# Decoder layer on one core: the opening's diagonal operands made early, its second rounds dense, its stores and loads in another order

## The chip, the core and the metric

One core of one Trainium2 chip runs the whole kernel. TensorE (PE) multiplies matrices into PSUM, VectorE (DVE), ScalarE (ACT) and GpSimd (POOL) work elementwise, and SyncE (SP) issues the DMA transfers. Each engine runs its own instructions in order and waits on semaphores for the others. The metric is the device time of one execution in microseconds (us), lower is better.

## The reference

The input `x` is (4, 2048, 512) in float32, with a context of 77 tokens for each of 4 batches. Three sublayers add to `x` in turn, each on its layer norm:

```python
x = x + recurrence(layernorm(x))            # diagonal state space along the FIRST axis, 4 steps, blocks of 64 features
x = x + cross_attention(layernorm(x), ctx)  # 16 heads of 32, 77 keys, softmax, output projection
x = x + ffn(layernorm(x))                   # 512 -> 2048, butterfly, gelu, butterfly, 2048 -> 512
```

A butterfly is a product of 11 sparse stages (2048 = 2^11), each mixing pairs of features at distance 1, 2, 4, ... 1024. It is linear, so the kernel multiplies `W_exp` with the up butterfly, and the down butterfly with `W_con`, once at the start, and has two dense matrices after that.

## The kernel before, in words

The second axis of `x` is cut into 16 tiles of 128 positions, each with all 4 steps of the first axis. A loop runs over the tiles: `feed_forward` of one tile is interleaved on TensorE with `front` of the next (recurrence, attention and three norms). Dense products use a scheme of seven products for a 2 x 2 block product; so each weight is stored as seven quarter-sized operands: three plain quarters and four sums, in DRAM tensors `up7` (8 blocks of hidden features), `dn7` (7 operands) and `wq7`.

Ahead of the loop stands the opening, which is where the change lies. It holds three generators, each of which emits some instructions up to its next `yield`; calls of `run(...)` (L783) and the loop at L802 decide which comes next. TensorE and SyncE run strictly in that written order (`manual_schedule`, L765). The order on VectorE, ScalarE and GpSimd is made by a planner that works with estimated times; only instructions under `keep` stay in order there.

- `taps` (L68) makes the recurrence matrices `gt`: four rounds, where each L111/L112 product waits for VectorE's L128 to L131.
- `keys` (L135) makes the keys (L146, evicted at L150) and values (L156).
- `prep` is `_prepare` (L220). It makes the two dense matrices. The up matrix: products of the low 7 stages (`_low_products`, L181) and of the high 4 stages (`_high_products`, L206), then a first round of products with the low stages (L282) into `wup`, transposes (L291) into `wdn`, and a second round with the high stages (L304), whose right operands are 16 "diagonals": 128 x 128 blocks that spread the high products over a mask (L244). The results go to `up7`: three plain quarters for each of 8 blocks are stored from `wup` (L326, 24 stores of 128 KB), and four sums made by GpSimd (L321, L323) and VectorE (L322, L324) in the buffer of `wo`, three slots in turn, are stored with one transfer each (L327, 8 stores of 512 KB). `W_con` is loaded (L310) into `wdn` as each group of the second round is done with it. The down matrix: a second round first (L340, with its own 16 diagonals), transposes (L350), low stages (L359), then sums (L370 to L373) and stores (L375) into `dn7`.
- `first` is `front(0)` (L495): the first tile's norm, recurrence, norm, seven query products `q` (L490), scores (L548), softmax (L552 to L558), transposes of the probabilities (L570), outputs (L580), seven output products `w` (L490), and the norm before the feed-forward (L446).

Buffers are shared by tags. `pt`, the transposed probabilities (L566), has the tag of the query weights `wq` (L777), so that the first copy into it (L575) has to wait until the store of `wq` (L801) has been read out. `wup` is overwritten by the second round of the down matrix, so an eviction there waits for the stores and sums that still read the up matrix. The feed-forward's buffers (`xlast`, `wts`, `ffn`, L820 to L822) lie where the opening's pool `prep` was, and the first of their users wait for all of that pool's last readers.

The pieces that the change touches and what calls them:

## Time and profile before

| | us |
|---|---|
| median of 3 runs (lowest, highest) | 2680.2 (2679.2, 2681.05) |
| the profiled execution's own time | 2681.39 |
| its span, first to last instruction | 2679.6 |
| first product of the feed-forward (L649) starts at | 265.69 |
| mean granted TensorE clock | 0.985 |

Busy times of the span: TensorE 2586.2 (97%), VectorE 1454.6 (54%), ScalarE 810.2 (30%), GpSimd 947.8 (35%). A line of a timeline reads: start, duration, engine, line of the kernel, operation, output<-inputs, shape, count, and in brackets the idle time of the engine just before and what ended it. A group's line gives busy time and the mean of one in ns. A chain's line gives start, duration and what it was. L12 is line 12 of the kernel before.

### The profile page before, as it was taken

How to read it: one execution, taken by the hardware profiler on the slowest of the kernel's cores; microseconds unless marked ns; L12 is line 12 of the kernel's file. 1: busy time of each engine (PE TensorE's matmuls, PEld its weight loads, DVE VectorE, ACT ScalarE, POOL GpSimd, SP SyncE). 2: the span in 40 equal slices, each digit the busy share in tenths (PEclk: the TensorE clock that was granted, in tenths of full speed). 3: DMA queues.
4: the chain of work that ended last, by engine and by line, in shares of the span. 5: the costliest groups of instructions: out<-in, count | busy, mean ns of one | idle time of the engine just before them, and what ended most of it. 6: DMA issues, size and time to landing. Idle time of an engine off the chain costs nothing.

```text
span 2679.6 us, 37402 instructions
## 1 busy us (share of the span) xinstructions
PE 2586.2 (97%) x14536; PEld 2197.8 (82%) x14536; DVE 1454.6 (54%) x3349; ACT 810.2 (30%) x1470; POOL 947.8 (35%) x1023
## 2 busy tenths in 40 slices
PE   7876999999999999999999999999999999999999
PEld 4755888888888888888888888888888888888888
DVE  5466555556455455645545654655555564554541
ACT  1322332414132332414133241413324141323321
POOL 4043252433425242342515234341524334252423
PEclk9978999999999999999999999999999999999999
DMA  5255324243332424233242423334242433324234
GB/s 176 81 169 175 128 92 159 93 156 108 105 139 91 162 95 158 91 134 130 85 148 94 171 93 118 130 103 146 93 158 93 156 108 105 140 91 146 95 128 139
DMA packets 92595, 333.60 MB, mean 124 GB/s; under 512 B 15362, under 2 KB 44162, under 8 KB 75266
## 3 DMA queue, kind: packets, MB, share of 16 engines
q1 hardware_dynamic: 92418, 331.21, 35.8%
q8 instruction: 116, 1.90, 0.3%
q14 instruction: 61, 0.49, 0.1%
HBM read 297.61 MB, written 33.57 MB: 124 GB/s over the span
## 4 chain that ended last, share of the span: by engine, by line
PE 82%; DVE 6%; ACT 4%; issue 1%; DMA 1%; SPq 0%; ACTq 0%; DVEq 0%
PE ps_a L716 12%; PE ps_b L649 10%; PE ps_b L716 8%; PE ps_w L490 7%; PE ps_a L649 7%; PE ps_c L649 7%; PE ps_q L490 7%; PE ps_c L716 6%; PE ps_sc L548 4%; PE ps_pt L570 4%; PE ps_s L505 3%; PE ps_o L580 2%; PE ps_t L446 2%; ACT L554 1%; ACT L654 1%; DVE st L411 1%
## 5 line engine op out<-in xcount | busy, mean ns | idle before, releaser
L649 PE MATMUL ps_b<-tb,w_up 128*128 128x256 f32 x1536 | 397.8, 380 | 0.0
L716 PE MATMUL ps_a<-w_dn,a 128*128 128x256 f32 x1536 | 373.0, 380 | 0.0
L692 POOL TENSOR_TENSOR s<-a,a 128x256 f32<-128x256 f32 x128 | 92.8, 725 | 676.7 <-ACT a L654 454.2
L649 PEld LDWEIGHTS ps_b<-tb,w_up 128*128 128x128 f32 x1536 | 288.0, 191 | 39.3 <-issue 0.2
L654 ACT ACTIVATE a<-a,hbias 128x256 f32<-128x256 f32 x384 | 193.6, 508 | 407.4 <-DVE a L687 277.6
L716 PEld LDWEIGHTS ps_a<-w_dn,a 128*128 128x128 f32 x1536 | 282.7, 190 | 41.3 <-issue 3.0
L649 PE MATMUL ps_a<-xnt,w_up 128*128 128x256 f32 x1024 | 263.9, 380 | 8.7 <-DMA w_up<-up 8.7
L716 PE MATMUL ps_c<-w_dn,s 128*128 128x256 f32 x1024 | 248.7, 379 | 0.0
L558 POOL TENSOR_TENSOR pr<-pr,sm 128x1232 f32<-128x1232 f32 x64 | 143.9, 2249 | 272.3 <-DVE sm L557 234.1
L447 ACT COPY xnt<-ps_t 128x512 f32<-128x512 f32 x128 | 73.5, 587 | 525.6 <-PE ps_t L446 525.6
L649 PEld LDWEIGHTS ps_a<-xnt,w_up 128*128 128x128 f32 x1024 | 191.9, 191 | 34.5 <-POOL ybias L819 9.1
L716 PEld LDWEIGHTS ps_c<-w_dn,s 128*128 128x128 f32 x1024 | 189.0, 190 | 27.5
L548 PE MATMUL ps_sc<-kbd,qt 128*128 128x308 f32 x512 | 176.3, 442 | 7.9 <-DVE pr L553 7.6
L598 DVE TENSOR_TENSOR xt<-ps_w,xt 128x512 f32<-128x512 f32 x96 | 66.1, 689 | 213.8 <-PE ps_w L490 144.9
L704 POOL TENSOR_TENSOR xt<-xt,ybias 128x256 f32<-128x256 f32 x128 | 99.2, 807 | 223.3 <-DVE xn L437 223.2
L570 PE MATMUL ps_pt<-ident,pr 128*77 128x128 f32 x1024 | 146.1, 279 | 9.5 <-ACT a L654 3.6
L570 PEld LDWEIGHTS ps_pt<-ident,pr 128*77 128x77 f32 x1024 | 118.8, 149 | 43.8 <-ACT a L654 11.0
L554 ACT ACTIVATE pr<-pr 128x308 f32<-128x308 f32 x256 | 111.6, 457 | 132.9 <-DVE pr L553 132.4
L490 PE MATMUL ps_q<-xnt,wq 128*128 128x256 f32 x640 | 151.3, 380 | 0.0
L490 PEld LDWEIGHTS ps_q<-xnt,wq 128*128 128x128 f32 x640 | 121.4, 190 | 16.2
L649 PE MATMUL ps_c<-tb,w_up 128*128 128x256 f32 x512 | 132.3, 381 | 0.0
L649 PE MATMUL ps_c<-xnt,w_up 128*128 128x256 f32 x512 | 131.5, 379 | 0.0
(202 smaller groups left out, 4531.2 us busy)
## 6 DMA issues: line engine op xcount, KB each, us to landing
w_up<-up SPq DMA_DIRECT2D x128, 896.0 KB, 4.6
w_dn<-dn SPq DMA_DIRECT2D x112, 1024.0 KB, 4.8
wq<-wq SPq DMA_DIRECT2D x16, 1792.0 KB, 8.4
xt<-in_x SPq DMA_DIRECT2D x16, 1024.0 KB, 5.4
out<-xt SPq DMA_DIRECT2D x64, 256.0 KB, 4.8
wdn<-in_wexp_t SPq DMA_DIRECT2D x4, 1024.0 KB, 10.3
wdn<-in_wcon SPq DMA_DIRECT2D x4, 1024.0 KB, 5.0
up<-wo SPq DMA_DIRECT2D x8, 512.0 KB, 3.9
```

The source lines that it names most:

```text
L447: nc.scalar.copy(xnt[:, :, t, :], ps)
L490: nc.tensor.matmul(tiles[key][:, r, :], lhsT=lhs(i, r, k), rhs=rhs(i, r, k), start=key == i and r == 0 and k == 0, stop=k == 1, skip_group ...
L505: nc.tensor.matmul(ps[:, 2 * i : T, f * NS : (f + 1) * NS], lhsT=xpt[:, i, c * (P // NS) + f, :], rhs=gt[:, 0 : T - 2 * i, :], start=i == ...
L548: nc.tensor.matmul(ps[:, 0 : 4 * NK], lhsT=qt[:, g, t, :], rhs=kbd[:, t, g, :], start=True, stop=True)
L554: nc.scalar.activation(pg, pg, AF.Exp, scale=1.0 / math.sqrt(DH))
L558: nc.gpsimd.tensor_tensor(pr, pr, sm.unsqueeze(2).to_broadcast([P, NH, NK]), ALU.mult)
L570: nc.tensor.transpose(pt_ps[0:NK, j, :], pr[:, 4 * g + j, :], ident)
L649: nc.tensor.matmul(ps, lhsT=w[:, c, :], rhs=rhs[i - 1][:, c], start=first and c == 0, stop=c == 1, skip_group_check=True)
L654: nc.scalar.activation(out, x, AF.Gelu, bias=hbias[:, b : b + 1])
L692: nc.gpsimd.tensor_tensor(s1, a21, a22, ALU.add)
L704: nc.gpsimd.tensor_tensor(r, r, ybias[:, d], ALU.add)
L716: nc.tensor.matmul(ps[:, t, :], lhsT=act[p][lhs[i]][:, t, :], rhs=w[:, p, :], start=first and p == 0 and t == 0, stop=p == h - 1, skip_gro ...
```

## The change

- The 16 diagonals of each matrix are made by one call, all at once: those of the up matrix ahead of the transposes L291, into the buffer of `wo`; those of the down matrix after the second round of the up matrix, into the buffer that held the keys' weights (tag `xt1`). The buffer `more` and the use of `ybias` for them go.
- The four groups of the second round L304 follow each other with nothing of `first` between. The second round L340 runs with its loops exchanged (`c` outside, `g` inside) and gives way to `first` after every group.
- The high products of both matrices and the low products of the down matrix move to earlier places; `low_dn` is loaded earlier.
- The 24 stores of plain quarters are all issued ahead of the sums and their 8 stores. The store of `wq` comes after those.
- The sums and stores of `dn7` are made in four parts of 2 blocks instead of two parts of 4 (stores of 256 KB).
- The loads at the start are reordered (`x` after the keys' operands and the low coefficients), the tile `x` of the second position is loaded earlier, and the steps of the three generators are interleaved in another order; one step of `prep` is now one group instead of four.
- The pools `ffn` and `wts` change places.

```diff
+    yield
...
-        yield
...
         pz = nxt
+        yield
...
     nc.sync.dma_start(out=wk, in_=wk_t.rearrange("(c p) e -> p c e", p=P))
+    yield
     nc.sync.dma_start(out=wv, in_=wv_t.rearrange("(c p) e -> p c e", p=P))
...
-    def diagonal(hp, m, place):
-        bd = place.rearrange("p (b i) -> p b i", b=NB)
-        keep(nc.vector.tensor_tensor(bd, hp[:, m, :].unsqueeze(2).to_broadcast([P, NB, sub]),
-                                     mask.unsqueeze(1).to_broadcast([P, NB, sub]), ALU.mult))
-        return bd.rearrange("p b i -> p (b i)")
+    def diagonals(hp, place):
+        for m in range(NB):
+            keep(nc.vector.tensor_tensor(place[:, m, :].rearrange("p (b i) -> p b i", b=NB),
+                                         hp[:, m, :].unsqueeze(2).to_broadcast([P, NB, sub]),
+                                         mask.unsqueeze(1).to_broadcast([P, NB, sub]), ALU.mult))
+        return [place[:, m, :] for m in range(NB)]
...
-        nc.sync.dma_start(out=high, in_=coefs)
+    for i, coefs in enumerate((up_high, dn_high)):
+        nc.sync.dma_start(out=highs[:, i], in_=coefs)
     half = NB * 2 * (P // 2 - 1)
     nc.sync.dma_start(out=low[:, 0:half], in_=up_low[:, 0:half])
     nc.sync.dma_start(out=low[:, half:nlow], in_=up_low[:, half:nlow])
+    yield
...
+    hp = _regrouped(nc, keep, pool, hscr[0], _high_products(nc, pool, highs[:, 0], False), "hp_up")
     e = _low_products(nc, keep, low, False, True)
-    hp = _regrouped(nc, keep, pool, hscr[0], _high_products(nc, pool, highs[0], False), "hp_up")
+    hp_dn = _high_products(nc, pool, highs[:, 1], True)
     yield
...
     nc.sync.dma_start(out=bias, in_=up_bias)
+    nc.sync.dma_start(out=brow[0:1, :], in_=brw.rearrange("o g x -> o (g x)"))
...
         yield
-    nc.sync.dma_start(out=brow[0:1, :], in_=brw.rearrange("o g x -> o (g x)"))
-    hp_dn = _regrouped(nc, keep, pool, hscr[1], _high_products(nc, pool, highs[1], True), "hp_dn")
+    nc.sync.dma_start(out=b2, in_=brow[0, :].rearrange("(p m) -> p m", m=NB))
+    low = pool.tile([P, nlow], F32, tag="lowc", name="low_dn")
+    keep(nc.sync.dma_start(out=low, in_=dn_low))
+    hp_dn = _regrouped(nc, keep, pool, hscr[1], hp_dn, "hp_dn")
+    bd = diagonals(hp, spare[:, 0 : NB * P].rearrange("p (m q) -> p m q", q=P))
...
-    low = pool.tile([P, nlow], F32, tag="lowc", name="low_dn")
-    keep(nc.sync.dma_start(out=low, in_=dn_low))
-    nc.sync.dma_start(out=b2, in_=brow[0, :].rearrange("(p m) -> p m", m=NB))
+    el = _low_products(nc, keep, low, True, False)
     pb = banks()
     for g in range(4):
-        bd = [diagonal(hp, 4 * g + j, room3[:, (4 * g + j) * P : (4 * g + j + 1) * P]) for j in range(4)]
         for c in range(NC):
...
                 nc.tensor.matmul(ps.rearrange("p (k m) -> p m k", m=4)[:, j], lhsT=t[:, 4 * g + j, c * P : (c + 1) * P],
-                                 rhs=bd[j], start=j == 0, stop=True, skip_group_check=True)
+                                 rhs=bd[4 * g + j], start=j == 0, stop=True, skip_group_check=True)
...
     nc.vector.tensor_copy(b2, pb[:, 0:NB])
-    nc.sync.dma_start(out=brow[1, :].rearrange("(p m) -> p m", m=NB), in_=b2)
+    bdd = diagonals(hp_dn, late())
     h, k = HID // 2, NC // 2
-    for p in range(NB // 2):
+
+    def quarters(p):
         q = slice(p * P, (p + 1) * P)
         a11, a12 = wup[:, 0:k, q], wup[:, k:NC, q]
         q = slice(h + p * P, h + (p + 1) * P)
-        a21, a22 = wup[:, 0:k, q], wup[:, k:NC, q]
-        s = room3[:, p % 3 * 1024 : p % 3 * 1024 + 1024].rearrange("p (i k q) -> p i k q", i=4, k=k)
-        nc.gpsimd.tensor_tensor(s[:, 0], a21, a22, ALU.add)
-        nc.vector.tensor_tensor(s[:, 1], s[:, 0], a11, ALU.subtract)
-        nc.gpsimd.tensor_tensor(s[:, 2], a11, a21, ALU.subtract)
-        nc.vector.tensor_tensor(s[:, 3], a12, s[:, 1], ALU.subtract)
+        return a11, a12, wup[:, 0:k, q], wup[:, k:NC, q]
+
+    for p in range(NB // 2):
+        a11, a12, a21, a22 = quarters(p)
         for i, a in enumerate((a11, a12, a22)):
             nc.sync.dma_start(out=up7[p][:, i], in_=a)
+    for p in range(NB // 2):
+        a11, a12, a21, a22 = quarters(p)
+        s = spare[:, p % 3 * 1024 : p % 3 * 1024 + 1024].rearrange("p (i k q) -> p i k q", i=4, k=k)
+        nc.gpsimd.tensor_tensor(s[:, 0], a21, a22, ALU.add)
+        nc.gpsimd.tensor_tensor(s[:, 2], a11, a21, ALU.subtract)
+        nc.vector.tensor_tensor(s[:, 1], s[:, 0], a11, ALU.subtract)
+        nc.vector.tensor_tensor(s[:, 3], a12, s[:, 1], ALU.subtract)
         nc.sync.dma_start(out=up7[p][:, 3:7], in_=s)
-        if p % 2:
-            yield
-    e = _low_products(nc, keep, low, True, False)
-    more = sums[0].tile([P, 8, P], F32, name="more")
-    places = [more[:, i] for i in range(8)] + [room4[:, i * P : (i + 1) * P] for i in range(4)]
-    places += places[0:4]
-    yield
-    for g in range(4):
-        bd = [diagonal(hp_dn, 4 * g + j, places[4 * g + j]) for j in range(4)]
-        for c in range(NC):
+        yield
+    nc.sync.dma_start(out=brow[1, :].rearrange("(p m) -> p m", m=NB), in_=b2)
+    for c in range(NC):
+        for g in range(4):
             ps = banks()
             for j in range(4):
                 nc.tensor.matmul(ps.rearrange("p (k m) -> p m k", m=4)[:, j], lhsT=t[:, 4 * g + j, c * P : (c + 1) * P],
-                                 rhs=bd[j], start=j == 0, stop=True, skip_group_check=True)
+                                 rhs=bdd[4 * g + j], start=j == 0, stop=True, skip_group_check=True)
             evict(wup[:, c, :].rearrange("p (k m) -> p k m", m=NB)[:, :, 4 * g : 4 * g + 4], ps.rearrange("p (k m) -> p k m", m=4))
-        yield
+            yield
...
-        nc.tensor.matmul(ps, lhsT=e[:, b, :], rhs=t[:, b, :], start=True, stop=True)
+        nc.tensor.matmul(ps, lhsT=el[:, b, :], rhs=t[:, b, :], start=True, stop=True)
         evict(wdn[:, b, :], ps)
-        if n % 2:
-            yield
         if n == h:
             nc.sync.dma_start(out=b1, in_=brow[1, :].rearrange("(b p) -> p b", p=P))
-        if n % h == h - 1:
-            f = slice(n // h * (h // 2), (n // h + 1) * (h // 2))
-            b11, b12, b21, b22 = (wdn[:, r * h + f.start : r * h + f.stop, c * (D // 2) : (c + 1) * (D // 2)].rearrange("p (x b) d -> p x b d", x=2)
+        if n % 4 == 3:
+            f = slice(n // 4 * 2, n // 4 * 2 + 2)
+            b11, b12, b21, b22 = (wdn[:, r * h + f.start : r * h + f.stop, c * (D // 2) : (c + 1) * (D // 2)]
                                   for r in range(2) for c in range(2))
-            t1, t2, t3, n4 = (wup[:, i, :].rearrange("p (x y) -> p x y", x=2)[:, :, n // h * D : (n // h + 1) * D] .rearrange("p x (b d) -> p x b d", b=2) for i in range(4))
+            t1, t2, t3, n4 = (wup[:, i, :].rearrange("p (x y) -> p x y", x=2)[:, :, f.start * P : f.stop * P] for i in range(4))
             nc.vector.tensor_tensor(t1, b12, b11, ALU.subtract)
             nc.gpsimd.tensor_tensor(t3, b22, b12, ALU.subtract)
             nc.vector.tensor_tensor(t2, b22, t1, ALU.subtract)
             nc.vector.tensor_tensor(n4, b21, t2, ALU.subtract)
             for i, w in ((0, b11), (1, b21), (2, b22), (4, t1), (6, t3), (5, t2), (3, n4)):
-                nc.sync.dma_start(out=dn7[i][:, f, :].rearrange("p (x b) d -> p x b d", x=2), in_=w)
+                nc.sync.dma_start(out=dn7[i][:, f, :], in_=w)
+        yield
     keep(nc.vector.tensor_tensor(bias, b1, bias, ALU.add))
     yield
...
-                        up_bias, dn_low, dn_high, wcon, wup, wdn, hbias, up7, dn7)
+        rooms = high, row, wo.rearrange("p i k d -> p (i k d)")
+        prep = _prepare(nc, tc.keep_in_program_order, pool, rooms, lambda: xpool.tile([P, NB, P], F32, tag="xt1", name="bd"),
+                        banks, dram, ident, wexp_t, up_low, up_high, up_bias, dn_low, dn_high, wcon, wup, wdn, hbias, up7, dn7)
         room = (work.tile([P, NC, T * NK], F32, tag="pr", name="ct"), xpool.tile([P, NC, D], F32, tag="xt1", name="wk"),
...
+            for g in gens:
+                next(g, None)
+
+        def quarter_loads(w, w_t, places):
+            src = w_t.rearrange("(c p) e -> p c e", p=P)
+            for i, (c, e) in zip(places, ((0, 0), (1, 0), (1, 1), (0, 1))):
+                nc.sync.dma_start(out=w[:, i], in_=src[:, 2 * c : 2 * c + 2, e * (D // 2) : (e + 1) * (D // 2)])
+
         with tc.tile_pool(name="taps", bufs=1) as tp:
             taps = _recurrence_taps(nc, tp, psum, ssm_vec, ssm_vt, ssm_vinv, gt)
+            run(taps, keys, prep, keys)
             xts[0] = load_x(0)
+            next(prep)
+            quarter_loads(wq, wq_t, (0, 1, 3, 6))
             first = front(0, xts.pop(0), ready, wq)
-
-            def run(*gens):
-                for g in gens:
-                    next(g, None)
-
-            run(taps, keys, prep)
-            src = wq_t.rearrange("(c p) e -> p c e", p=P)
-            for i, (c, e) in ((0, (0, 0)), (1, (1, 0)), (3, (1, 1)), (6, (0, 1))):
-                nc.sync.dma_start(out=wq[:, i], in_=src[:, 2 * c : 2 * c + 2, e * (D // 2) : (e + 1) * (D // 2)])
-            run(first, keys, keys, taps, keys, keys, taps, keys, keys, taps, taps)
-        sums.append(stack.enter_context(tc.tile_pool(name="sums", bufs=1)))
-        run(first, keys, first, keys, first, first, prep, first, first, first, first)
+            run(keys, keys, taps, keys, taps, first, keys, taps, keys, taps, keys, first, keys, first)
+            run(prep, first, keys, first, first)
+        run(first, first, first, first)
         nc.gpsimd.tensor_tensor(wq[:, 4], wq[:, 6], wq[:, 3], ALU.add)
         nc.gpsimd.tensor_tensor(wq[:, 6], wq[:, 0], wq[:, 6], ALU.subtract)
         nc.gpsimd.tensor_tensor(wq[:, 5], wq[:, 4], wq[:, 0], ALU.subtract)
         nc.gpsimd.tensor_tensor(wq[:, 2], wq[:, 1], wq[:, 5], ALU.subtract)
-        run(prep, prep, first, prep, first, first, prep, first, first)
+        run(prep, prep, first, prep, first, prep, first)
+        run(prep, first, prep, first, prep, first, prep)
         run(prep, prep, prep, prep)
-        run(first, first, first, prep, first, first, prep, first, first, prep, first, first, prep)
+        for _ in range(8):
+            run(first, prep)
         nc.sync.dma_start(out=wq7, in_=wq)
+        run(first, first, first)
         for n, _ in enumerate(prep):
-            for _ in range(1 + (n < 4)):
+            if n % 3 != 2 or n > 14:
                 next(first, None)
-            if n == 4:
-                src = wo_t.rearrange("(c p) e -> p c e", p=P)
-                for i, (c, e) in ((0, (0, 0)), (1, (1, 0)), (2, (1, 1)), (6, (0, 1))):
-                    nc.sync.dma_start(out=wo[:, i], in_=src[:, 2 * c : 2 * c + 2, e * (D // 2) : (e + 1) * (D // 2)])
+            if n == 3:
+                quarter_loads(wo, wo_t, (0, 1, 2, 6))
                 nc.gpsimd.tensor_tensor(wo[:, 4], wo[:, 6], wo[:, 0], ALU.subtract)
                 nc.gpsimd.tensor_tensor(wo[:, 6], wo[:, 2], wo[:, 6], ALU.subtract)
                 nc.gpsimd.tensor_tensor(wo[:, 5], wo[:, 2], wo[:, 4], ALU.subtract)
                 nc.gpsimd.tensor_tensor(wo[:, 3], wo[:, 1], wo[:, 5], ALU.subtract)
-        xts[1] = load_x(1)
+            if n == 18:
+                xts[1] = load_x(1)
         for _ in first:
             pass
         db = work.tile([P, D], F32, tag="xn", name="db")
@@ -818,8 +829,8 @@
         nc.sync.dma_start(out=db, in_=down_bias.partition_broadcast(P))
         nc.gpsimd.tensor_tensor(ybias, ybias, db, ALU.add)
     xlast = ctx.enter_context(tc.tile_pool(name="xlast", bufs=1))
+    ffn = ctx.enter_context(tc.tile_pool(name="ffn", bufs=2))
     wts = ctx.enter_context(tc.tile_pool(name="wts", bufs=3))
-    ffn = ctx.enter_context(tc.tile_pool(name="ffn", bufs=2))
```

## The prediction

> **What bounds the kernel now.** I read the page's slices first: TensorE stands at 9 tenths everywhere but in the first three or four of the 40 slices (67 us each), so the loop over the 16 tiles is TensorE's, and only the opening, up to the first product of the feed-forward at 265.69 us, has room. From that product on both programs run the same instructions in the same order, except that the second tile's first transposes move. So I cut the opening into six stages by TensorE's order and asked for busy time by stage (columns: stretch, length, then PE, PEld, DVE, ACT, POOL busy, granted clock, DMA share, GB/s):
>
> ```profile
> 0.00:58.20 58.20, 40.74 (x153) 24.92 (x154) 27.49 (x119) 5.85 (x10) 29.23 (x82) 0.97 0.60 200
> 58.20:86.98 28.78, 28.78 (x249) 27.04 (x248) 18.34 (x39) 19.36 (x27) 1.03 (x1) 1.00 0.27 83
> 86.98:135.50 48.52, 37.62 (x217) 32.86 (x217) 19.55 (x39) 10.14 (x17) 5.45 (x6) 0.86 0.19 66
> 135.50:209.86 74.36, 52.35 (x346) 40.02 (x346) 46.56 (x82) 15.44 (x29) 34.77 (x30) 0.72 0.45 152
> 209.86:243.67 33.81, 33.42 (x154) 22.95 (x152) 19.48 (x27) 11.42 (x21) 7.12 (x4) 1.00 0.35 110
> 243.67:265.69 22.02, 3.77 (x17) 3.04 (x17) 18.28 (x44) 2.92 (x5) 7.44 (x6) 0.65 0.96 320
> ```
>
> Call them A (taps, keys, recurrence), B (first round, transposes), C (second round of the up matrix, L304), D (attention with the down matrix's second round, L340), E (its transposes and last products) and F (last stores, first weights). B and E are full; A, C, D and F have holes. In C the timeline shows whose:
>
> ```profile
> 103.77 3.84 PE L304 MATMUL ps_p<-wo,wdn 128*128 128x128 f32 x32 [0.98 <-DVE wo L244]
> 107.45 0.95 PE L309 MATMUL ps_p<-b,wo 128*128 128x1 f32 x8
> ...
> 113.03 3.81 PE L304 MATMUL ps_p<-wo,wdn 128*128 128x128 f32 x32 [1.07 <-DVE wo L244]
> ...
> 126.44 0.71 PE L304 MATMUL ps_p<-wo,wdn 128*128 128x128 f32 x4 [3.48 <-DVE wo L244]
> ```
>
> Each group of four blocks waits for its diagonals (L244), then takes 4.46 us (113.03 to 117.49, L309 included). The costs of a diagonal, by group on VectorE in 120 to 210 us:
>
> ```profile
> L244 DVE TENSOR_TENSOR more<-hp_dn,mask 128x128 f32<-128x128 f32 x12 | 9.9, 883 | 0.0
> ...
> L244 DVE TENSOR_TENSOR ybias<-hp_dn,mask 128x128 f32<-128x128 f32 x4 | 0.9, 284 | 0.0
> ```
>
> Alone four take 0.9 us; beside a GpSimd operation one takes 0.9. In D the attention starts late for another reason, which the timelines of the DMA queue and VectorE and the table of transfers show (start, us, instruction):
>
> ```profile
> 135.28 0.42 SPq L801 DMA_DIRECT2D wq<-wq  x1
> 146.33 2.05 SPq L326 DMA_DIRECT2D up<-wup  x3
> 145.45 0.69 DVE L575 COPY pt<-ps_pt 77x512 f32<-77x512 f32 x1 [0.25 <-DMA up<-wup]
> wq<-wq SPq DMA_DIRECT2D x1, 1792.0 KB, 10.1
> ```
>
> `pt` lies in `wq`'s buffer, so the first copy of transposed probabilities (L575) can't run before the store of `wq` (L801) has landed: 135.28 + 10.1 = 145.4. In F the chain is one of stores and loads:
>
> ```profile
> 244.62 3.12 DVE wup L370
> ...
> 250.37 6.52 DMA dn<-wup
> ...
> 257.35 8.34 DMA w_up<-up
> ```
>
> **The change part by part.** Times from the start of a stage.
>
> **A, 58.2 to 51.5.** `x` (1 MB) leaves the head of the queue: the keys' operands come about 3 us sooner, and their products run first, at 8.3 instead of 12.9 us. One key product (3 us) now stands between each recurrence step and the next tap, hiding the three waits of 2.03, 2.03 and 1.07 us for L130. Against it: the second row of `xp` takes `high`'s buffer, free only after GpSimd's last L206, which waits behind the `wq` loads (36.5 us, same bytes as before): about 41 us, a hole of 2. Sum -6.7.
>
> **B, 28.8 to 30.3.** All 16 diagonals of the up matrix go to VectorE just before the evictions of L291: 16 x 0.22 = 3.6 us, of which the free PSUM banks cover some two: +1.5. Loading `low_dn` and its products (9.2 us of GpSimd) come here and into C; GpSimd was idle there, and evictions from PSUM took 0.69 us beside these products in D (176.24), so they cost nothing.
>
> **C, 48.5 to 17.8.** Four groups of 4.46 us, no diagonals, no attention between: -30.7. Six of the seven `q` products and the first scores, which lay in C, are only moved on into D.
>
> **D, 74.4 to 91.** The long one; offsets from its start.
> - VectorE makes the 16 down diagonals while GpSimd does six L321/L323 (0.73) and L534 (1.26), 5.7 us. The Trainium skill ("SBUF — State Buffer", SBUF: two separate sides) says that the pair of ports is locked for a whole instruction and a VectorE operation with two SBUF inputs blocks. Row: 0.93 us a diagonal beside GpSimd (3.86 for four at 183.75), not 0.22. By the row nine diagonals and the first `q` sum end at 7.6, where by uncontended rows it would be 3; by the rule, full blocking, 9. I take the row. The later products wait for these sums in one PSUM tile: scores start at 16, two rows of four at 0.97 each end at 25 with the row sum (1.44).
> - Queue: 24 stores of plain quarters now stand ahead of the eight stores of sums. Three took 2.05, so 24 x 0.70 = 16.8, plus 2 behind the last `wcon` load: the first sums' store goes at 19 and lands 3.9 later. GpSimd: L558 of row 0 from 23.2 to 25.5, three pairs of sums to 30, L558 of row 1 to 35.5, two last pairs to 38.3; last L324 at 39.0, its store at 39.2, and only then L801 at 39.8. It needs 8 us (10.1 in the crowded queue, 8.4 for the load of that size; 5 at the peak of 437 GB/s; I take the nearest): 48.
> - Behind that wait: VectorE's and ScalarE's first `pt` copies, hence everything in their queues. From the same copy to the last row sum took 145.45 to 170.31 = 24.9 us; less ten L322/L324 (5.5), plus three evictions (2.1): 21.5, so 69.5.
> - Left for TensorE: two rows of transposes and outputs (6.0), eight groups of L340 (7.5), two `w` products (3.5), copies waited for (1.5): 88.
> - The clock: the skill ("TensorE: Matmul & The Clock Gate", Part 1) says that after an idle window of about 3.4 us the array runs at half speed until busy as long. D is emptier than before. Row: 0.72 granted in D. By the rule alone the last 18 us would double at worst (+18), by the row +7; a burst of L340 (3.83 us for 32, as warm) shows that it recovers, so I take +3: 91.
> - Loads of `wo` queue behind L801 and land at about 51; their four sums (1.26 each) end at 56, before L558 of row 2 (59): hidden by 3 us.
>
> **E, 33.8 to 39.5.** TensorE has 31 us left, two `w` products being done, and the four transposes of `xn` come in. But the last L598 ends at 17, and between it and the first `xn` row VectorE's queue now holds 12 us: six L411 at 0.65 (the second tile's among them), four evictions at 0.69, one and a half quarters' sums and the Newton steps. `xn` comes at 29.5, then 10 us of products: 39.5. Before, this norm lay in F under the stores.
>
> **F, 22.0 to 15.5.** Half-size sums: last eviction 0.6, three of 0.69 beside one GpSimd 1.26: 3.3 (before 5.6). The last store has 256 KB: 3.5, as the 128 KB ones took, instead of 6.52. `x` no longer precedes `w_up`: 4.6 is the median of its loads, but the second tile's four transposes, which wait for GpSimd's L819, now stand first: 8.1. These (2.4 us) leave the loop.
>
> **Other places for weights**: nothing; the first `w_up` still waits for every last `dn7` store, in either layout.
>
> New opening 51.5 + 30.3 + 17.8 + 91 + 39.5 + 15.5 = 245.6, against 265.7: -20.1, with the moved transposes -22.5. From the span 2679.6 that gives 2657.1. The profiled run took 2681.4, the median is 2680.2, so I add 0.6 to a span: **2658**.
>
> **The rivals.**
> - *The store queue becomes the bound (slower).* At 139.48 three such stores took 6.27 us behind L801. For: eight outstanding transfers are all the queue has. Against: L801 no longer lies among them. At 2.1 us each, 24 take 50: D grows by 33 and the kernel ends at 2691. It decides from 1.6 us a store (24 x 0.9 = 22). Chance 0.12.
> - *D and E are nearer to their parts.* If the sums run ahead, L801 goes at 33, and if the norm's instructions fit between evictions (E 34): 16 less, from 2628 to 2645, centre 2640. For: VectorE was busy only 63% of D. Chance 0.22.
> - *The gain comes back in D.* Clock by its row, `wo` sums late before L558, D at 103 to 108: 2672 to 2680. For: clock 0.72. Chance 0.16.
> - *It doesn't do what it says*: if the diagonals were not the reason for C's holes, C stays at 26 or so: inside the first range.
>
> **How the numbers follow.** 0.2% (5.4 us, about what a measurement tells from no change) puts "same" at 2675 to 2686. My case, 2645 to 2672, has 0.50: faster. The second is faster. Of the third half is faster, half same. The first is slower, the same slowness also coming from smaller mishaps of its kind. Faster 0.80, same 0.08, slower 0.12. Range 2632 to 2682: below it about 0.07, above 0.12.
>
> **What would show it.** Right: L304 in one run of about 18 us without waits for L244; L272 near 51; L801 issued some 40 us after the last L309, with the first L575 waiting for it; the first `w_up` product near 246. Wrong: L801 landing before 42 or after 55; a clock under 0.6 in D; no stall on `xn` in E; C over 22.

## The result, and the profile after

The changed kernel takes 2663.98 us (median of 4 runs, 2662.71 to 2665.23) against 2680.2 us: a ratio of 0.994, with a 95% interval of 0.9922 to 0.9957. That is 16 us faster; 2658 (2632 to 2682) was forecast. Its profiled span is 2662.7 us (before 2679.6), at a granted TensorE clock of 0.987 (before 0.985).

The code of the changed kernel stands up to twelve lines lower. The lines that matter below, before > after: taps L116 > L117 and L124 the same (VectorE's read of `ps_g`, TensorE's product `ps_ri`), keys L146 > L148, start of the first round L272 > L277, the diagonals L244 > L248 (L244 is now ScalarE's eviction), second rounds L304 > L310 and L340 > L346, the bias products L309 > L315, plain quarters' stores L326 > L331, sums' stores L327 > L339, transposes and low stages of the down matrix L350 and L359 > L356 and L365, its sums L370 to L373 > L374 to L377 and stores L375 > L379, scores L548 > L553, GpSimd's softmax product L558 > L563, first copy of `pt` L575 > L580, store of `wq` L801 > L812, addition of the biases L819 > L830, first feed-forward product L649 > L654.

The same cut of the opening into stages A to F by TensorE's order, busy time by stage of the changed kernel (columns as before: stretch, length, PE, PEld, DVE, ACT, POOL busy, granted clock, DMA share, GB/s):

```profile
0.00:59.15 59.15, 43.62 (x153) 25.23 (x153) 33.80 (x119) 5.75 (x10) 28.94 (x82) 0.91 0.59 197
59.15:89.23 30.08, 28.88 (x250) 27.17 (x250) 21.80 (x56) 19.55 (x28) 3.78 (x5) 1.00 0.26 79
89.23:107.01 17.78, 17.78 (x162) 17.78 (x161) 4.86 (x8) 6.21 (x11) 8.58 (x6) 1.00 0.53 179
107.01:192.99 85.98, 55.06 (x418) 43.84 (x418) 51.84 (x97) 19.86 (x37) 32.16 (x29) 0.84 0.40 133
192.99:234.47 41.48, 34.64 (x153) 23.62 (x151) 30.89 (x75) 12.51 (x22) 5.84 (x4) 0.88 0.46 145
234.47:253.14 18.67, 5.03 (x19) 3.74 (x20) 10.85 (x14) 2.93 (x5) 10.67 (x11) 0.58 1.01 327
```

| stage | before | predicted | after | after minus predicted |
|---|---|---|---|---|
| A | 58.2 | 51.5 | 59.2 | +7.7 |
| B | 28.8 | 30.3 | 30.1 | -0.2 |
| C | 48.5 | 17.8 | 17.8 | 0 |
| D | 74.4 | 91 | 86.0 | -5.0 |
| E | 33.8 | 39.5 | 41.5 | +2.0 |
| F | 22.0 | 15.5 | 18.7 | +3.2 |
| from the first L654 to the end | 2413.9 | 2411.5 | 2409.6 | -1.9 |

So C became dense and D longer, as forecast, and the total is near; but A gained nothing. Before, TensorE had three waits for L130 in A, of 2.03, 2.03 and 1.07 us; here the first of them and what follows it:

```profile
22.96 0.43 PE L111 MATMUL ps_g<-vt,pz_next 64*128 64x64 f32 x2 [2.03 <-DVE ti L130]
...
23.70 6.10 PE L146 MATMUL ps_k<-ct,wk 128*128 128x308 f32 x16
29.74 0.43 PE L122 MATMUL ps_rr<-pz_next,vt 64*64 64x128 f32 x2
```

In the changed kernel TensorE's timeline shows new waits, and VectorE's timeline what it did in the meantime:

```profile
19.77 0.40 PE L124 MATMUL ps_ri<-pz,vt 64*64 64x128 f32 x2 [1.43 <-DVE gt L117]
25.25 0.40 PE L124 MATMUL ps_ri<-pz_next,vt 64*64 64x128 f32 x2 [1.43 <-DVE gt L117]
25.80 4.03 PE L148 MATMUL ps_k<-ct,wk 128*128 128x308 f32 x8
33.33 0.66 PE L124 MATMUL ps_ri<-pz_next,vt 64*64 64x128 f32 x2 [2.33 <-DVE gt L117]
34.34 6.24 PE L158 MATMUL ps_v<-wv,ct 128*77 128x512 f32 x8
```

```profile
17.21 1.94 DVE L152 COPY kbd<-ps_k 32x308 f32<-32x308 f32 x4 [0.83 <-PE ps_k L148]
19.16 0.46 DVE L117 TENSOR_SCALAR gt<-ps_g 64x64 f32<-64x64 f32 x2
```

The three waits for L130 are gone, and three for L117 (5.19 us together, against 5.13) stand in their place. `ps_g`, `ps_rr` and `ps_ri` share one PSUM tag with two buffers. So `ps_ri` needs the one that VectorE still has to read for `ps_g`, and that read stands behind the key product's four copies (the third time with the norm's small steps between them). Before, a key product (23.70 above) lay between `ps_g` and `ps_rr` and hid the read; the moved `yield` puts it behind `ps_ri`. The products after the second and third wait ran at half clock (4.03 against 2.34 us for the same eight, 6.24 against 3.60).

In D, the timelines of the DMA queue and of VectorE show the order that was forecast, somewhat earlier:

```profile
106.88 15.15 SPq L331 DMA_DIRECT2D up<-wup  x24
122.17 21.45 SPq L339 DMA_DIRECT2D up<-wo  x8
143.66 0.44 SPq L812 DMA_DIRECT2D wq<-wq  x1
```

```profile
151.44 0.69 DVE L580 COPY pt<-ps_pt 77x512 f32<-77x512 f32 x1 [8.21 <-DMA wq<-wq]
```

The store of `wq` goes 36.7 us after D's start and lands at 151.4, which is what the first copy of `pt` waits for, and TensorE waits for the copies:

```profile
152.12 1.99 PE L575 MATMUL ps_pt<-ident,pr 128*77 128x128 f32 x8 [16.30 <-ACT pt L578]
```

In E the transposes of `xn` wait 6.69 us for VectorE (221.44). In F VectorE's timeline has two waits on the way to the first product:

```profile
242.86 1.80 DVE L624 TENSOR_TENSOR tb<-xnt 128x512 f32<-128x512 f32 x1 [4.60 <-DMA ybias<-in_b_con]
...
248.15 3.11 DVE L469 TENSOR_SCALAR xp<-xt,mv,y 128x256 f32<-128x256 f32 x4 [1.16 <-POOL ybias L830]
```

The first is the opening's pool coming free with the last stores (the first `w_up` is issued at 242.56). The bracket names the load of `ybias`, but that lands only 4.8 us after its issue at 239.35; what had just landed is the last store (242.3). The second is the second tile's rows `xp`: the bias `db` lies in one of the two buffers that they use, until L830 has read it. The last transpose is at 251.40, the first L654 at 253.14.

### The profile page after: what moved, and what is told of

The parts are those of the page before. It is cut to its first block, busy times and chain, and to the rows that moved or that the text cites. A ratio compares the mean times of both kernels' runs of the same rounds, so it can differ in the third digit from the quotient of the medians.

```text
span 2662.7 us, 37427 instructions
## 1 busy us (share of the span) xinstructions
PE 2570.4 (97%) x14536; PEld 2183.1 (82%) x14536; DVE 1453.5 (55%) x3355; ACT 810.1 (30%) x1470; POOL 949.7 (36%) x1025
## 4 chain that ended last, share of the span: by engine, by line
PE 83%; DVE 6%; ACT 4%; issue 1%; DMA 0%; POOL 0%; SPq 0%; ACTq 0%; DVEq 0%; POOLq 0%
PE ps_a L721 13%; PE ps_b L654 10%; PE ps_b L721 8%; PE ps_w L495 7%; PE ps_a L654 7%; PE ps_c L654 7%; PE ps_q L495 7%; PE ps_c L721 6%; PE ps_sc L553 5%; PE ps_pt L575 4%; PE ps_s L510 3%; PE ps_o L585 2%; PE ps_t L451 2%; ACT L559 1%; DVE st L416 1%
## 5 line engine op out<-in xcount | busy, mean ns | idle before, releaser
L654 PE MATMUL ps_b<-tb,w_up 128*128 128x256 f32 x1536 | 396.8, 379 | 0.0
L654 PEld LDWEIGHTS ps_b<-tb,w_up 128*128 128x128 f32 x1536 | 287.4, 190 | 39.3
L654 PE MATMUL ps_a<-xnt,w_up 128*128 128x256 f32 x1024 | 263.6, 380 | 0.0
L563 POOL TENSOR_TENSOR pr<-pr,sm 128x1232 f32<-128x1232 f32 x64 | 144.0, 2250 | 263.0 <-DVE sm L562 259.0
L654 PEld LDWEIGHTS ps_a<-xnt,w_up 128*128 128x128 f32 x1024 | 191.7, 191 | 25.7
L709 POOL TENSOR_TENSOR xt<-xt,ybias 128x256 f32<-128x256 f32 x128 | 99.3, 810 | 223.0 <-DVE xn L442 222.9
L553 PE MATMUL ps_sc<-kbd,qt 128*128 128x308 f32 x512 | 172.6, 434 | 5.1 <-DVE pr L558 4.8
L575 PE MATMUL ps_pt<-ident,pr 128*77 128x128 f32 x1024 | 145.7, 278 | 29.0 <-ACT pt L578 17.8
L575 PEld LDWEIGHTS ps_pt<-ident,pr 128*77 128x77 f32 x1024 | 118.9, 149 | 61.7 <-ACT pt L578 26.4
L654 PE MATMUL ps_c<-xnt,w_up 128*128 128x256 f32 x512 | 131.5, 379 | 0.0
L654 PE MATMUL ps_c<-tb,w_up 128*128 128x256 f32 x512 | 131.5, 379 | 0.0
```

Of the source, the lines that this page charges most:

```text
L553: nc.tensor.matmul(ps[:, 0 : 4 * NK], lhsT=qt[:, g, t, :], rhs=kbd[:, t, g, :], start=True, stop=True)
L563: nc.gpsimd.tensor_tensor(pr, pr, sm.unsqueeze(2).to_broadcast([P, NH, NK]), ALU.mult)
L575: nc.tensor.transpose(pt_ps[0:NK, j, :], pr[:, 4 * g + j, :], ident)
L654: nc.tensor.matmul(ps, lhsT=w[:, c, :], rhs=rhs[i - 1][:, c], start=first and c == 0, stop=c == 1, skip_group_check=True)
L709: nc.gpsimd.tensor_tensor(r, r, ybias[:, d], ALU.add)
```

## The experiments

Each kernel is the changed one with one edit (g_bank_hp has two, the combos three or four), timed against the kernel before. Ratios have an interval of about 0.0013 to either side (0.0007 for dn_diag_group, 0.0018 for the changed kernel). Stages come from TensorE's timeline of each profile, cut at the same instructions as above, but with C up to the end of the last L315, which lies 0.14 us later. Kernels with moved lines have their own numbers in their rows.

| kernel | median us | ratio to before | A | C | D | E | F | rest |
|---|---|---|---|---|---|---|---|---|
| changed | 2663.98 | 0.9940 | 59.1 | 17.9 | 85.8 | 41.5 | 18.7 | 2409.6 |
| g_bank | 2658.25 | 0.9915 | 52.3 | 17.9 | 89.5 | 40.7 | 18.7 | 2409.1 |
| g_bank_hp | 2657.10 | 0.9912 | 50.2 | 17.9 | 87.2 | 40.6 | 18.6 | 2409.5 |
| diag_group | 2667.79 | 0.9953 | 57.5 | 20.6 | 87.4 | 40.7 | 18.5 | 2409.3 |
| wq7_early | 2649.96 | 0.9886 | 60.5 | 17.9 | 73.9 | 40.7 | 18.7 | 2409.3 |
| wq7_mid | 2648.01 | 0.9879 | 59.6 | 17.9 | 70.3 | 40.8 | 18.6 | 2409.2 |
| dn_diag_group | 2674.77 | 0.9978 | 58.9 | 17.9 | 103.2 | 41.2 | 18.6 | 2409.4 |
| dn_halves | 2670.98 | 0.9967 | 59.1 | 17.9 | 85.8 | 42.2 | 24.9 | 2409.1 |
| xt1_late | 2666.13 | 0.9942 | 60.8 | 17.9 | 86.0 | 38.9 | 15.3 | 2415.4 |
| pools | 2663.59 | 0.9937 | 58.6 | 17.9 | 87.0 | 40.5 | 18.5 | 2409.2 |
| combo | 2633.30 | 0.9827 | 50.8 | 17.9 | 71.4 | 40.5 | 14.4 | 2406.6 |
| combo_x24 | 2636.59 | 0.9836 | 50.9 | 17.9 | 71.6 | 39.7 | 18.0 | 2406.4 |
| combo_mid | 2632.89 | 0.9818 | 50.6 | 17.9 | 69.9 | 41.2 | 14.6 | 2405.6 |

Stage B is 30.1 in all but diag_group (31.0, its cut lying after the first wait for diagonals). A comes out between 57.5 and 60.8 where nothing in it was edited.

### Where A's gain went: g_bank, g_bank_hp

```diff
-        ps = psum.tile([P, 512], F32, tag="f", name="ps_g")
+        ps = psum.tile([P, 512], F32, tag="c", name="ps_g")
```

> The changed kernel, with the tap product ps_g in the PSUM tag 'c' instead of 'f' (two buffers, shared by ps_g, ps_rr and ps_ri), so that ps_ri need not wait until VectorE has read ps_g. Theory (that wait ate the 6.7 us of stage A): TensorE's waits of 1.43, 1.43 and 2.33 us for L117 go, and with them the cold key and value products (4.03 instead of 2.34, 6.24 instead of 3.6 us); TensorE then comes to the first transposes of xp at about 39 instead of 48.0 and stands there until the second row of xp, which needs the buffer of the high coefficients (44.4). L277 begins near 55.5 instead of 59.2, the kernel takes some 3.6 us less than the changed one: 2660. Rival (the loads of x, wv and wdn set the pace, not PSUM): the waits are taken over by others at the same places, L277 stays within 1 us of 59, 2664.

TensorE's timeline of g_bank, at the third of the three places and at the end of A:

```profile
26.00 0.38 PE L124 MATMUL ps_ri<-pz_next,vt 64*64 64x128 f32 x2
...
52.26 3.65 PE L277 MATMUL ps_p<-low_up,b 128*1 128x128 f32 x32
```

L124 has no bracket: it waits for nothing, nor does it at 17.60 and 22.13. All three waits are gone and A is 52.3. Shorter ones stand before the next tap products instead (0.45, 1.40 and 0.21 us, for L131 and the norm's small steps on VectorE), as the rival said, but they come to 2.1 us and the clock stays at 1.00 through A. The hole for `xp` was smaller than expected (0.95 and 0.89 us), so this came out better than the theory: one PSUM buffer is worth 6.9 us of A between these two profiles. By the ratios the kernel gains 6.7 us (0.0025 of 2680).

g_bank_hp also puts the high coefficients elsewhere:

```diff
...
-        high = work.tile([P, 2, HIGH, NB // 2, 4], F32, tag="xn", name="high")
+        spare = wo.rearrange("p i k d -> p (i k d)")
+        high = spare[:, 3072:3328].rearrange("p (a b c d) -> p a b c d", a=2, b=HIGH, c=NB // 2)
```

> As g_bank, and the high coefficients lie in the unused end of wo's buffer instead of one of xn's two, so that no row of xp waits for GpSimd's last product of them. Theory: the hole before the transposes is gone too, L277 begins at 51 to 52 (the 51.5 of the prediction) and the kernel takes 7 to 8 us less than the changed one: 2656.5. Rival: the next wait (value weights, the low products, a cold clock) holds L277 at 55 or later, 2660.

A is 50.2, a little below the prediction's 51.5, with no hole before the transposes. The further 2 us of A are in the profile; in the medians the step from g_bank (1.2 us) is within the scatter.

### What the early diagonals of the up matrix are worth: diag_group

```diff
...
-    bd = diagonals(hp, spare[:, 0 : NB * P].rearrange("p (m q) -> p m q", q=P))
...
+    bd = []
     for g in range(4):
+        bd += diagonals(hp, spare[:, 0 : NB * P].rearrange("p (m q) -> p m q", q=P), range(4 * g, 4 * g + 4))
```

> The changed kernel, with the 16 up diagonals again made four at a time at the head of each group of L310 (in the same places), as before the change; nothing else. It asks how much of the 30.7 us that stage C lost came from the early diagonals, and how much from the seven q products and scores that were only moved on to D. Prediction's reading (L310 waits for L248 as it did before, some 3.5 us a group): C grows from 17.8 by 10 to 14, B shrinks by 1.2, kernel 8 to 12 us longer, 2672 to 2676. Rival (most of C's gain is moved work; alone four diagonals take 0.9 us and wait only behind one eviction): C grows by 3 x 1.5 = 4.5, B shrinks by 1.2, kernel 3 us longer, 2667.

TensorE's timeline of diag_group in the first group, and the first four diagonals on VectorE's:

```profile
88.44 0.68 PE L311 MATMUL ps_p<-wo,wdn 128*128 128x128 f32 x4 [1.77 <-DVE wo L248]
90.68 3.39 PE L311 MATMUL ps_p<-wo,wdn 128*128 128x128 f32 x28 [1.56 <-DVE wo L248]
```

```profile
87.31 3.52 DVE L248 TENSOR_TENSOR wo<-hp_up,mask 128x128 f32<-128x128 f32 x4
```

With 0.20 and 0.28 us ahead of two later groups the waits sum to 3.8 us. From the start of B, which loses its 16 diagonals, to the next `q` product it takes 51.4 us (57.47 to 108.86) instead of 47.9 (59.15 to 107.01), 3.5 us more, as by the ratios (0.0013 of 2680): the rival is right. Of the 30.7 us that C lost, 19.8 are TensorE's attention work moved on to D (37.6 busy less 17.8), and 10.9 were idle, 8.3 of it waits for the diagonals. With the groups following each other, 3.8 of these remain even where the diagonals are made late; making them early takes those, 3.5 us net. The first four, beside GpSimd, took 3.52 us, the last four 0.89. Here is one of the first four, with GpSimd's operation at that time:

```profile
88.22 2.25 POOL L183 TENSOR_TENSOR low_dn<-low_dn 128x1024 f32<-128x1024 f32 x1
88.42 2.21 DVE L248 TENSOR_TENSOR wo<-hp_up,mask 128x128 f32<-128x128 f32 x1
```

The diagonal starts while that operation runs and ends 0.15 us after it, so it waits out one GpSimd operation and no more. All 14 profiles show the same: of their 448 diagonals 76 took over 0.3 us, and each of these ended 0.14 to 0.15 us after a GpSimd operation that had been running at its start; the other 372 took 0.23 to 0.29 us, and none of them started inside one.

### What the place of one store costs: wq7_early, wq7_mid

```diff
+        nc.sync.dma_start(out=wq7, in_=wq)
         run(prep, prep, prep, prep)
         for _ in range(8):
             run(first, prep)
-        nc.sync.dma_start(out=wq7, in_=wq)
```

> The changed kernel, with the store of wq to wq7 (L812) moved ahead of the four groups of L310 instead of behind the sums of the up matrix; nothing else. Theory (stage D waits for this store): it lands in stage C, the first copy of transposed probabilities no longer waits 8.21 us for it and comes near 131 instead of 151.4; then GpSimd sets the pace (the four sums of wo, which land near 148, stand ahead of the third row's L563, at 153 to 155 instead of 164.5), so D shortens by about 9 us and the kernel by as much: 2655 (between 4 and 14 us less). Rival (the store is hidden by GpSimd's or TensorE's own work): under 2 us less, 2662 to 2665. Second rival (the early store delays the loads of wcon and with them the 16 diagonals or L340): slower than the changed kernel.

D shrinks by 11.9 us, the kernel by 14.5 (0.0054 of 2680): the store was on the path. wq7_mid has the same line behind the call of four `prep` instead, its place of before the change:

> The changed kernel, with the store of wq where it was before the change: behind the last L310 group, right ahead of the 24 stores of plain quarters. It asks what the change itself lost by moving it behind the stores of sums, beside what an even earlier place gives (wq7_early: D 73.9 instead of 85.8). Theory (any place ahead of the 24 stores frees pt in time, as GpSimd hands over the first row only at about 129): it lands by 118, D is 74 to 79, 2650 to 2655. Rival (eight outstanding transfers: the 24 stores, and the sums' stores behind them, come some 6 us later, the sums' three places stay full and GpSimd and the loads of wo are late): D 80 to 86, 2657 to 2663.

The DMA queue, TensorE and GpSimd in wq7_mid:

```profile
107.29 0.38 SPq L810 DMA_DIRECT2D wq<-wq  x1
107.77 19.24 SPq L331 DMA_DIRECT2D up<-wup  x24
127.13 20.22 SPq L339 DMA_DIRECT2D up<-wo  x8
```

```profile
129.74 3.97 PE L575 MATMUL ps_pt<-ident,pr 128*77 128x128 f32 x16 [1.19 <-POOL pr L563]
```

```profile
133.88 2.25 POOL L563 TENSOR_TENSOR pr<-pr,sm 128x1232 f32<-128x1232 f32 x1 [4.19 <-issue]
```

The transposes of the first row run on without the wait of 16.3 us. The first store of sums goes 5 us later (127.13 instead of 122.17), as the rival said, and GpSimd waits twice some 0.6 us for a free place, but no more: the planner put GpSimd's second row (133.88, in the changed kernel 137.16) ahead of the sums. So the change itself lost some 16 us (0.0061 of 2680) by moving this store behind the sums, as much as it gained in all.

### What the early diagonals of the down matrix are worth: dn_diag_group

```diff
...
-    bdd = diagonals(hp_dn, late())
+    room = late()
+    bdd = []
...
-    for c in range(NC):
-        for g in range(4):
+    for g in range(4):
+        bdd += diagonals(hp_dn, room, range(4 * g, 4 * g + 4))
+        for c in range(NC):
```

> The changed kernel, with the down matrix's 16 diagonals made four at a time at the head of each group of four L346 blocks, the blocks in the order of before (for each group its four columns), everything else as changed. It asks what the early down diagonals are worth in stage D (86.0 us). Theory (a large part of the 64.4 us that before needed after its first copy of pt, against 41.5 now, is L340 waiting for diagonals, and VectorE's rows waiting behind them): the scores start 2 us sooner, but three groups of TensorE wait for four diagonals each, and D grows by 5 or more in all, kernel 2669 to 2675. Rival (as in the up matrix, where making them early was worth 2 us: the time after pt is won by VectorE and GpSimd having finished the sums of the up matrix before): D within 2 us, kernel 2662 to 2666.

The stretch from the first row's later transposes to the first L356, with the same 344 products, in the changed kernel and then in dn_diag_group:

```profile
152.12:192.99 40.87, 35.89 (x344) 31.02 (x345) 22.89 (x39) 13.73 (x26) 15.95 (x12) 0.96 0.05 17
```

```profile
150.76:210.16 59.40, 48.17 (x344) 39.46 (x345) 29.15 (x55) 13.71 (x26) 16.14 (x12) 0.73 0.04 12
```

It is 18.5 us longer. TensorE's idle time grows from 5.0 to 11.2 us, and its timeline has just these 6.25 us as seven waits of 0.25 to 1.51 us for L248. The other 12.3 us are busy time: the same products at a granted clock of 0.73 instead of 0.96, for instance three blocks of L348 in 4.74 us, which took 2.84. The median of 21 runs is 10 us above the changed kernel (0.0038 of 2680), with times from 2669 to 2681, so this profiled execution is the longest of them. Before the change, the stretch from the first `pt` copy (145.45) to the first L350 took 64.4 us, with TensorE busy 47.0 and a clock of 0.72, so this part undone gives back most of what was won there. Here the theory holds, unlike in C: early diagonals pay where their waits would lie between short products. The order of the blocks went back with them (a column at a time needs all 16 diagonals at once), and the two are not told apart.

### The second half of the opening: dn_halves, xt1_late, pools

dn_halves makes the sums and stores of the down matrix in halves again, with slices and stores twice as large:

```diff
-        if n % 4 == 3:
-            f = slice(n // 4 * 2, n // 4 * 2 + 2)
+        if n % h == h - 1:
+            f = slice(n // h * (h // 2), (n // h + 1) * (h // 2))
...
```

> The changed kernel, with the down matrix's operands summed and stored in two halves instead of four quarters; nothing else. Theory (F is a chain from the last eviction through sums, last store, and what its landing releases): sums 5.6 instead of 3.1 us and the last store longer (6.52 against about 3.2), F grows by 5 us, kernel 2669. Rival (seven fewer issues on the queue and shorter work for VectorE in E give part of it back): 2 us or less, 2664 to 2666.

VectorE's timeline of dn_halves, at the end of the wait in F:

```profile
250.01 0.69 DVE L624 TENSOR_TENSOR tb<-xnt 128x512 f32<-128x512 f32 x1 [8.39 <-DMA dn<-wup]
```

The sums take 5.8 us, from 235.12 to 240.89 (3.1 in quarters), and from their end to the pool coming free 9.1 (5.3): F grows by 6.2 and the kernel by 7 (0.0027 of 2680). The theory holds.

```diff
-            if n == 18:
-                xts[1] = load_x(1)
+        xts[1] = load_x(1)
```

> The changed kernel, with the load of the second tile's x again behind all of the down matrix's stores, as before the change. Theory (the second tile's statistics on VectorE lie ahead of the first tile's xn, and its four transposes ahead of the first product): xn comes some 3.5 us sooner (three L416 of 0.68 and the small steps), so E is 3.5 shorter; L654 stands first in F and begins when its weights land, at least 3 us sooner; the loop takes the 2.4 us of transposes back: kernel 4 us shorter, 2660. Rival (loading x early is what the loop gained: from the first L654 to the end it took 2409.6 us against 2413.9 before): the loop grows by 4.4 or more, and the 1 MB load delays w_up in F: kernel the same or up to 3 us longer.

E is 2.6 and F 3.4 us shorter, as the theory said, and the time from the first L654 to the end is 5.8 longer, as the rival said: the sum is nothing. The early load moves six microseconds across the boundary.

pools:

```diff
+    wts = ctx.enter_context(tc.tile_pool(name="wts", bufs=3))
     ffn = ctx.enter_context(tc.tile_pool(name="ffn", bufs=2))
-    wts = ctx.enter_context(tc.tile_pool(name="wts", bufs=3))
```

> The changed kernel, with the pools of the loop's weights and of the feed-forward's activations again in the order of before (the weights' places first). Theory (the first w_up waits for the last dn7 store to land in either layout): F within 0.5 us of 18.7, kernel 2664 within its scatter of 2. Rival (the places decide what a weight load must wait for): F and the kernel differ by 2 us or more, in either direction.

No difference: F 18.5, kernel 2663.59.

### The repairs together: combo, combo_x24, combo_mid

combo has the edits of g_bank_hp and wq7_early, and one more:

```diff
-        db = work.tile([P, D], F32, tag="xn", name="db")
+        db = work.tile([P, D], F32, tag="pr", name="db")
```

> Both repairs together and a third: g_bank_hp (opening's waits for L117 and for the high coefficients' buffer), wq7_early (the store of wq before the second round), and the down bias read into a buffer of pr instead of xn, so that the rows of xp of the second tile need not wait in F until GpSimd has added it (L830). Theory (the three lie in stages A, D and F, one behind the other, and add up): 8 for the first, 14 for the second and some 5 for the third: 27 us less than the changed kernel, 2637. Rival (F's first product waits for its weights, not for xp): 22 less, 2642. Second rival (D's gain depends on A's timing): 2648 or more.

2633.3 us, 4 less than expected. The parts add up: A 50.8, D 71.4, F 14.4, and TensorE's timeline now has the weights as the last thing that the first product waits for:

```profile
225.07 1.10 PE L654 MATMUL ps_a<-xnt,w_up 128*128 128x256 f32 x4 [2.36 <-DMA w_up<-up]
```

The rest is 3 us shorter too (2406.6), since all 32 of the second tile's first recurrence products (L510, 215.64 to 222.7) now run in F's hole. That the moved bias buffer does this alone was not tried apart from the others.

```diff
-            if n == 18:
+            if n == 24:
                 xts[1] = load_x(1)
```

> combo, with the load of the second tile's x six steps later, between the stores of the second and the third quarter of the down matrix, so that its statistics lie behind the first tile's xn on VectorE. Theory (E's stall of 6.69 us on xn is VectorE's queue): xn comes 3 us sooner, E is 37.5 instead of 40.5, F stays at 14.4, since its first product waits for w_up and not for xp: 2630. Rival (the 1 MB load comes between the quarters' stores, and the second tile's rows late): F grows by what E loses, 2633 to 2636.

The wait on `xn` shrinks from 6.69 to 4.94 us and E by 0.8, but F grows by 3.6: the second tile's rows come late (TensorE's transposes at 217.34 wait 7.21 us for L469). The rival is right, and F takes back more than E loses.

> combo, with the store of wq at its place of before the change (as wq7_mid) instead of ahead of the second round; nothing else. Theory (wq7_mid's D of 70.3 against wq7_early's 73.9 comes from GpSimd, which takes the second row's L563 at once instead of behind two pairs of sums, and does so here too): D 68 to 70 instead of 71.4, 2630 to 2632. Rival (combo's D already has that row early enough, or the third row waits for the sums of wo instead): same as combo, 2632.5 to 2635.

D is 69.9, as the theory said, but E is 41.2, and the kernel's 2632.89 us is no different from combo. Both beat both kernels; the ratio to before is 0.9818 (0.9805 to 0.9832) for combo_mid.

## Why the prediction was right, and where not

**The total** was near by luck: two misses of opposite sign nearly cancelled, A (+7.7) against D (-5.0) and the loop (-1.9); E and F add 5.2. From the predicted span of 2657.1 all of them together lead to the 2662.7 measured. Of the signs named beforehand, C's single run of 17.8 us and the store of `wq` with the wait of `pt` came; the end of A near 51 (59.2) and the first product near 246 (253.1) did not; none of the signs of being wrong came.

**A, "hiding the three waits": this step failed.** It held that a key product between each recurrence step and the next tap takes the waits away. I looked at the wait that the move removes and not at what the key product had been hiding where it stood. The waits came back at L124 with the same sum, and g_bank shows that the PSUM buffer was their cause. The earlier start was also only partly there: the first key product began at 9.96, not 8.3, when its weights landed. The "hole of 2" for `high`'s buffer didn't show in the changed kernel, since TensorE came to it late; it was 1.8 us in g_bank.

**B and C** came as worked out (30.1 and 17.8). C's price of a group was right. Of the two reasons that it names together, no diagonals and no attention between, diag_group separates the first: 3.5 us net.

**D, right in its mechanism, most of its terms too long.** The first sum of `q` ended after 4.5 us instead of 7.6: GpSimd had begun its sums at 105.3, before the diagonals, so they overlapped for 2.5 us and not for 5.7; four of nine diagonals met one of its operations, and the nine took 3.62. Scores began at 12.3 (predicted 16), the 24 stores took 15.15 (16.8 and 2 more), `wq`'s store went at 36.7 (39.8) and landed after 7.8 (8). From the first `pt` copy to the last row sum it took 24 us (21.5), and the rest 17.6 (18.5 and 3 for the clock): TensorE was at full clock from 155.6 on. The 0.93 us a diagonal that the prediction took from a row is no rate: diag_group shows one diagonal waiting for the end of one GpSimd operation, of whatever length. The rule of the Trainium skill that the prediction quotes ("SBUF — State Buffer", SBUF: two separate sides), a lock for a whole instruction, says just that and agrees with all 14 profiles; the prediction took it for blocking through all of GpSimd's 5.7 us and set it aside for that. (Its 5 us for 1792 KB at 437 GB/s is 4.2; nothing rested on it.)

**E**: the stall on `xn` is there. `xn` came at 27.9 (29.5), but the products behind it took 13.6 us instead of 10, the granted clock being 0.50 from 217.1 to 227.3.

**F**: sums 3.1 (3.3), from there to the pool coming free 5.3 (3.5), then 10.3 to the first product (8.1), because the second tile's rows also waited for L830 and then ran beside GpSimd's L709 (3.11 us for four instead of some 1.4).

**The rivals.** The store queue was not the bound: 0.63 us a store, and still no harm at 0.80 in wq7_mid. The eight transfers that this rival names can be counted before the change: from L801 (135.28) on, the ninth, a store at 145.39, waits 1.9 us until `wq` has landed. D was 5 us nearer to its parts, E was not. The gain didn't come back in D through a cold clock. Places for weights: nothing, as said.

**The sum by undoing.** In ratios of 2680 us, undoing costs 3.5 (up diagonals, near the scatter), 10 (down diagonals, with their order) and 7 (quarters), nothing for the load of the second tile's `x` and for the pools; the store's place gives 16 back. Of the some 32 us gained beside that one line, this leaves about 12 to parts that were not undone. What the other moves (attention out of C, high and low products early) bring alone was not tried, and the parts need not add up.

## What to carry to other kernels

When a piece of work is moved to hide a wait, look for what it hid where it stood: count the buffers of every tag between the two places, and follow who must read each before the next is written. A store that frees a shared buffer belongs where its data is ready, not behind stores that wait for sums: look for the first writer of that buffer and ask when it would otherwise be ready. Price VectorE products such as the diagonals, beside GpSimd, by the length of the GpSimd operations that will be under way, one for each product. Cut the time by stages and undo one part at a time: here a gain of 16 us was one of some 30 less a loss of 16 by one line.

## What the runs showed of the hardware

Short waits cost more than their length. In the changed kernel's stage A, waits of 1.43 us (at 23.8) and 2.33 us (at 31.0) were each followed by a granted clock of 0.50, for 3.4 and 6.8 us; another of 1.43 us (at 18.3) was not. Cut where the clock changes, the stage shows a reason (PE's busy time is the second number behind the stretch, the clock stands third from the right):

```profile
15.68:19.09 3.41, 2.65 (x14) 1.68 (x12) 2.52 (x6) 0.00 (x0) 3.41 (x21) 1.00 1.05 390
19.09:22.51 3.42, 2.74 (x12) 1.84 (x12) 1.79 (x7) 0.00 (x0) 3.26 (x12) 1.00 0.80 125
22.51:25.92 3.41, 1.98 (x14) 1.45 (x14) 3.05 (x8) 0.00 (x0) 3.25 (x3) 1.00 0.87 300
25.92:29.33 3.41, 3.41 (x7) 2.32 (x8) 3.09 (x10) 0.00 (x0) 2.15 (x1) 0.50 1.03 399
```

In each of the 14 profiles all changes of the clock lie a whole number of 3.41 us apart, wherever the waits lie. The wait at 18.3 is split between two such windows, which are busy 2.65 and 2.74 us, and the clock stays; the one at 23.8 lies in one, which is busy 1.98 us, and the next window runs at half. In the first 290 us of the 14 profiles each of the 67 falls came after a window in which TensorE was busy 61% or less, and each of the 67 returns after one of 89% or more. Not every such window changed the clock.

How long the clock then stays at half differs between executions of the same code. After the 16 us wait in D, the changed kernel (first product at 152.12) and g_bank (145.16) run the same products. Full clock came back at 155.6 in the one, 3.5 us after the first product, and at 157.5 in the other, 12.4 us after it. g_bank's windows before that:

```profile
147.28:150.70 3.42, 3.42 (x40) 2.94 (x34) 0.69 (x1) 0.49 (x1) 2.89 (x3) 0.50 0.00 0
150.70:154.11 3.41, 2.38 (x6) 1.15 (x6) 1.47 (x4) 0.62 (x2) 2.14 (x2) 0.50 0.00 0
154.11:157.53 3.42, 3.40 (x10) 2.72 (x11) 1.71 (x5) 0.85 (x3) 0.00 (x0) 0.50 0.00 0
```

The second has a wait of 1.05 us; why the first, busy throughout, did not bring the clock back stays open. From the first product to the first L356 g_bank takes 44.6 us and the changed kernel 40.9, and the difference is busy time (39.6 against 35.9); g_bank's D of 89.5 is longer than the changed kernel's 85.8 for this reason. The Trainium skill ("TensorE: Matmul & The Clock Gate", Part 1) gives one window of about 3.4 us for either step, a window that runs freely. The length and the free running agree with these profiles; that the window is an idle one for the fall does not (58% busy at 22.51), nor that one busy window is always enough for the return, and the measurements decide. D took 85.8 to 89.5 us in the seven kernels that leave it alone, so a stage like it can't be priced to better than some 4 us.
